# Two bottleneck blocks: relus of the last stage's first tile between the products, its last row in two halves, and the order of columns and quarters in the Gram stage

## Chip, cores and metric

The kernel runs on one core of one Trainium2 chip. The metric is the device time of one execution in microseconds; three executions of the kernel before took 1890.41, 1890.45 and 1893.24 us, with a median of 1890.45 us.

## What is computed

Two residual bottleneck blocks in a row on a batch of 64 images with 1024 channels of 14 x 14 pixels, in float32, with batch statistics:

```python
out = relu(bn(conv1x1(x, w1), g1, be1))      # 1024 -> 256 channels
out = relu(bn(conv3x3(out, w2), g2, be2))    # 256 -> 256
out = bn(conv1x1(out, w3), g3, be3)          # 256 -> 1024
x = relu(x + softplus(residual_scale)[0] * out)
```

`bn` takes mean and variance over the batch and all pixels, so every normalization needs a whole layer before it can begin.

## The kernel before

A tile is two images: 128 partitions by 8 slices of channels (`CS`) by 392 pixels (`PX`); there are 32 tiles (`T`). The 256 channels in the middle of a block stay in SBUF (`y_all`, two slots of 128). Each block runs as: first 1x1 convolution, 3x3 convolution, a stage that finds the statistics of the third convolution, and the third convolution with the residual. In the second block the statistics come from the Gram matrix of `y` (`gram`, line 1315, and `conv3_stats`, line 1747), and the third convolution is the last stage (`residual`, line 1804, and `final`, line 1834). The change lies in these two.

Four engines work in parallel, each through its own queue in order: TensorE (PE) multiplies, VectorE (DVE) and ScalarE (ACT) normalize, copy and add, GpSimd (POOL) adds and issues some transfers, SyncE (SP) issues most transfers. `matmul` (line 160) and `act` (line 335) are helpers, so all matmuls show line 160 and most of ACT's work line 335. Both pin their instruction to the order of the program; what isn't pinned is placed by a scheduler.

**Gram stage.** `gram` builds products of pixel-major pieces of `y`. A group of 256 pixels is turned either by TensorE (`by_tensor`, 1389: four transposes into PSUM, then a copy to a tile `zt`; it serves the three groups of the piece `turned`, 768 pixels) or by DVE (`by_vector`, 1408, with STREAM_TRANSPOSE at 1307; it serves the eight pieces in `moved`). DVE turns only 32 x 32 blocks, so a moved piece is first spread over partitions by transfers into a buffer `home` (`move`, 1377, on SP and POOL) and, for the blocks that keep their partitions, by four copies on ACT (`stay`, 1370). Before any of that a piece is normalized by ACT (`normed`, a relu with scale and shift) and has a constant subtracted by DVE (`less`, 1348, through `center` at 1346). The first two moved pieces go by quarters (`quarter_comes`, 1413): normalized, centred and moved one after the other, so that the first transfers start early. The generator `pairs` (1420) writes this order out by hand. First come tile 0 and the four products of the last stage's first tile that fit into PSUM (`conv3_begun`, `conv3`); then the columns of `turned` and the quarters; then one `yield` for each group of 256 pixels, after which `gram_products` (1286) multiplies the group before it.

**Last stage.** Tile 0's eight products (`made`) exist before the scales do: four were put into `z` and four lie in PSUM banks. `residual` adds each to `x_0` with DVE (line 1813: product times scale plus `x`) and lets ACT do the relu; then one store of `x_0` on POOL's queue. Tiles 1 to 30 follow in pairs, four units each (`Conv3Pair`, 652), by a scheme with seven products in place of eight (`Seven`, 246; `stream`, 290). The first two units are started together: `p1` of both, then `p2`, `p6`, `p5`, `p6`, `p7`. After `p1`, `p6` and `p7` ACT copies the bank `y` (tag `cy`) into a tile `cu`, and the next product adds into that bank after the copy has read it. After `p2` and `p5` DVE adds the bank `cx` or `cp` to `x` (line 532), and `p3` adds into `cp` after that. POOL adds the copies to `x` (555 and 663), ACT and DVE do the relus (`end`, 665, and `go_out`, 670), and SP stores each unit's slices (675). `x_6` uses the buffer of `x_0`, so its load on SP waits for `x_0`'s store. Tile 31 comes last, again through `residual`: eight products of 392 columns, each followed by DVE and a relu on ACT, stores of two slices and, for the last two, of one slice each.

Of the kernel before, what the change touches and what calls it, by code (L numbers as in the profile page):

```python
# [18 lines left out]
CS = C // P  # L19
MS = M // P  # L20
G = 2
# [49 lines left out]
def bottlenecks(ctx: ExitStack, tc: tile.TileContext, x, w1s, w2s, w3s, pars, out):  # L71
# [429 lines left out]
    class Conv3(Seven):  # L501
# [25 lines left out]
        def part(self, row, i):  # L527
            return self.xt[:, self.o[row], i * self.n : (i + 1) * self.n]
# [786 lines left out]
    def gram(psum, pool, homes, z, aff, minus_c, w3, beside):  # L1315
# [44 lines left out]
        def quarter(k, i):  # L1360
            a, e = moved[k]
            n = (e - a) // 4
            return a + i * n, a + i * n + n

        def home(k):
# [44 lines left out]
            turn(zt, home(k)[0], i * CH)  # L1410
            return zt

        def quarter_comes(k, i):
            normed(*quarter(k, i))
            less(*quarter(k, i))
            move(k, (i,))
# [387 lines left out]
    def residual(psum, xt, b, t, w3, aff, made=(), later=None):  # L1804

        scale, shift = aff
        to = mids[t] if b == 0 else out[t]
        tail = b == 1 and t == T - 1
        first = CS // 2 if b == 1 and t == 0 else 0
        for n, o in enumerate((*range(first, CS), *range(first))):  # L1810
            ps = made[o] if o < len(made) else conv3(psum, t, o, w3)
            v = xt[:, o, :]
            nc.vector.scalar_tensor_tensor(v, ps, scale[:, o : o + 1], v, ALU.mult, ALU.add)  # L1813
            relu = partial(act, v, v, AF.Relu, bias=shift[:, o : o + 1])
            if later is not None and o + 2 >= CS:
                later.append(relu)
            else:
                relu()

            step = CS if not tail else 1 if o + 2 >= CS else 2  # L1820
            if (n + 1) % step == 0:
                o = n
                queue = nc.scalar if o + 1 == CS and tail else nc.gpsimd if step == CS and b else nc.sync
                store = partial(
                    queue.dma_start,
                    out=to[:, (o + 1 - step) * PX : (o + 1) * PX],
                    in_=xt[:, o + 1 - step : o + 1, :].rearrange("p s f -> p (s f)"),
                )
                if later is not None:
                    later.append(store)  # L1830
                else:
                    store()

    def final(psum, pool, xpool, xs, a, w3, aff):


        units = []

        def pairs():
            for t in range(1, T - 1, 2):  # L1840
                ys = [[two(t + i, s) for i in range(2)] for s in range(MS)]
                sums = column_sums(pool, ys, PX, (2,))
                for q in range(CS // 2):
                    units.append(Conv3Pair(psum, pool, xs[t : t + 2], q, PX, ys, sums, w3, aff, out[t : t + 2]))
                    yield units[-1]

# [12 lines left out]

    def fused(psum, pool, one, right, coming, xs, raw, w1, w3, aff, par, stats, border, begun):  # L1860

# [323 lines left out]
    for b in range(2):  # L2185
# [9 lines left out]
        with tc.tile_pool(name=f"last_{b}", bufs=1, **({"reuse_waits": "tile"} if b == 0 else {})) as one, tc.tile_pool(  # L2195
# [12 lines left out]
            with ExitStack() as scope:  # L2208
# [41 lines left out]
                later = None if b else []  # L2250
                residual(psum, xs[0], b, 0, w3, aff, made, later)
                if b == 1:
                    more = scope.enter_context(tc.tile_pool(name="last_more", bufs=1, reuse_waits="tile"))
                    xs.append(load_x(more, b, len(xs), run=tc.keep_in_program_order))
                with tc.tile_pool(name=f"rest_{b}", bufs=1) as pool:
                    if b == 1:
                        final(psum, pool, [x_left] * 5 + [more], xs, w3, *weights, aff)
# [44 lines left out]
```

## Time and profile before

| | |
|---|---|
| runs | 1890.41, 1890.45, 1893.24 us, median 1890.45 us |
| the profiled execution | 1891.91 us, span from first to last instruction 1890.1 us |
| TensorE matmul busy | 1869.9 us (99%) |
| DVE, ACT, POOL busy | 1574.5 us (83%), 1106.6 us (59%), 740.0 us (39%) |
| TensorE's granted clock over the span | 0.998 |
| Gram stage of block 2 | 1509 to 1574 us of the span |
| last stage | 1588 to 1890 us of the span |

Times in the profile are microseconds from the span's start. A row of the timeline has start, duration, engine, line, operation, `out<-in` by tile names with the buffer numbers left out, shapes and a count; in brackets stand the idle time ahead of it on its engine and what ended that. Rows with a count are merged. A busy TensorE can still be at half clock; the table by stretches tells the clock that was granted.

### The profile page before, as it was taken

The numbers are of one execution on the slowest core, as the hardware profiler recorded it, in microseconds if no ns is written. First come the engines' busy times: TensorE is split into PE (matmuls) and PEld (weight loads), VectorE is DVE, ScalarE is ACT, GpSimd is POOL, SyncE is SP. The second block draws the span as 40 slices with busy tenths as digits, with TensorE's granted clock in tenths as the row PEclk, the third lists the DMA queues.
The fourth block names the chain that finished last, engine by engine and source line by source line (L and its number), as shares of the span: only waits on it lengthen the run. The fifth ranks groups of instructions, "written<-read, shape, count | busy, mean of one in ns | idle before, by whom it ended". The sixth has DMA issues, their size and how long they took to land. (4 is left out here: it accounts for less than half of the span.)

```text
span 1890.1 us, 28589 instructions
## 1 busy us (share of the span) xinstructions
PE 1869.9 (99%) x9748; PEld 1559.8 (83%) x9748; DVE 1574.5 (83%) x2498; ACT 1106.6 (59%) x2304; POOL 740.0 (39%) x762
## 2 busy tenths in 40 slices
PE   9999999999999999999999999999999999999999
PEld 5555557999998998899999999999999986555555
DVE  5787867999998776788788787899999986888886
ACT  2222214677777665555555555457777793666666
POOL 0111100211205655376776777311121151666664
PEclk9999999999999999999999999999999999999999
DMA  7777644787865556778787889468788376899997
GB/s 289 273 251 272 214 181 139 206 218 213 211 202 164 185 168 216 258 267 318 276 286 279 306 283 286 189 195 218 208 215 221 130 183 255 294 347 342 341 338 280
DMA packets 263186, 459.17 MB, mean 243 GB/s; under 512 B 59361, under 2 KB 229569, under 8 KB 249857
## 3 DMA queue, kind: packets, MB, share of 16 engines
q1 hardware_dynamic: 224784, 375.37, 59.5%
q0 software_dynamic: 31408, 29.30, 7.9%
q10 hardware_dynamic: 6848, 52.67, 6.8%
q8 instruction: 77, 1.26, 0.3%
q14 instruction: 69, 0.56, 0.1%
HBM read 289.44 MB, written 141.03 MB: 228 GB/s over the span
## 5 line engine op out<-in xcount | busy, mean ns | idle before, releaser
L160 PE MATMUL columns<-v,ub 128*128 128x224 f32 (+1 forms) x1536 | 302.9, 339 | 1.3 <-ACT columns L335 0.8
L335 ACT ACTIVATE x<-x,shift 128x392 f32<-128x392 f32 x452 | 259.8, 614 | 75.0 <-DVE x L532 31.4
L160 PEld LDWEIGHTS columns<-v,ub 128*128 128x128 f32 x1536 | 268.5, 188 | 8.0 <-ACT columns L335 1.5
L335 ACT ACTIVATE cu<-cy,scale 128x196 f32<-128x196 f32 (+1 forms) x360 | 175.6, 500 | 168.9 <-PE cy L160 161.9
L160 PE MATMUL ay<-at,ws 128*128 128x196 f32 (+1 forms) x760 | 191.5, 383 | 0.4 <-DVE at L453 0.2
L532 DVE SCALAR_TENSOR_TENSOR x<-cp,scale,x 128x196 f32<-128x196 f32 (+1 forms) x240 | 124.7, 520 | 50.6 <-PE cp L160 49.3
L160 PEld LDWEIGHTS ay<-at,ws 128*128 128x128 f32 x760 | 134.9, 190 | 35.5 <-ACT au L335 0.5
L663 POOL TENSOR_TENSOR x<-x,cu 128x392 f32<-128x392 f32 x120 | 125.6, 1047 | 73.9 <-DVE x L532 73.3
L335 ACT ACTIVATE au<-ay 128x196 f32<-128x196 f32 (+1 forms) x139 | 53.5, 385 | 169.7 <-PE ay L160 159.7
L160 PE MATMUL l<-diffs,ub 128*128 128x224 f32 (+1 forms) x768 | 149.7, 337 | 0.5 <-DVE diffs L801 0.3
L160 PE MATMUL m<-sums,ua 128*128 128x224 f32 (+1 forms) x752 | 146.0, 336 | 1.2 <-issue 0.6
L160 PEld LDWEIGHTS l<-diffs,ub 128*128 128x128 f32 x768 | 134.5, 189 | 1.7 <-DVE diffs L801 0.7
L160 PEld LDWEIGHTS m<-sums,ua 128*128 128x128 f32 x752 | 131.4, 189 | 2.6 <-issue 1.0
L1102 POOL DMA_DIRECT2D y<-f x24 | 32.2, 1644 | 256.3 <-DVE f L1001 256.3
L160 PE MATMUL cx<-y,w 128*128 128x196 f32 (+1 forms) x400 | 123.7, 395 | 0.0
L555 POOL TENSOR_TENSOR x<-x,cu 128x196 f32<-128x196 f32 (+1 forms) x120 | 104.5, 871 | 48.4 <-ACT cu L335 31.2
L160 PE MATMUL cy<-y,w 128*128 128x196 f32 (+1 forms) x372 | 116.1, 399 | 1.8 <-ACT y L335 0.9
L335 ACT ACTIVATE y<-y,shift,scale 128x320 f32<-128x320 f32 (+8 forms) x111 | 111.9, 1036 | 7.1 <-DVE shift L2055 6.4
L560 POOL TENSOR_TENSOR x<-x,cu 128x392 f32<-128x392 f32 x60 | 80.3, 1338 | 85.1 <-DVE x L532 83.6
L207 POOL DMA_DIRECT2D u<-y x48 | 26.0, 543 | 210.9 <-ACT y L335 210.1
L160 PE MATMUL cy<-ct,ws 128*128 128x392 f32 x240 | 100.7, 503 | 3.7 <-ACT cu L335 3.7
L1904 POOL TENSOR_SCALAR y<-y,scale 128x392 f32<-128x392 f32 x57 | 92.3, 1620 | 28.5 <-DVE scale L2245 28.5
(317 smaller groups left out, 4522.0 us busy)
## 6 DMA issues: line engine op xcount, KB each, us to landing
ub<-u SPq DMA_DIRECT2D x92, 768.0 KB, 5.7
x<-in_x SPq DMA_DIRECT2D x35, 1568.0 KB, 8.1
x<-mid SPq DMA_DIRECT2D x32, 1568.0 KB, 8.2
out<-x SPq DMA_DIRECT2D x123, 392.0 KB, 7.0
mid<-x ACTq DMA_DIRECT2D x30, 1568.0 KB, 8.6
x<-in_x SPq DMA_DIRECT2D x108, 392.0 KB, 7.9
ua<-u SPq DMA_DIRECT2D x92, 256.0 KB, 3.2
z<-kept SPq DMA_DIRECT2D x60, 392.0 KB, 2.9
```

Source lines behind the costliest of these rows:

```text
L160: tc.keep_in_program_order(nc.tensor.matmul(*args, **kw))
L207: nc.gpsimd.dma_start(out=us[b][i][:, s, o], in_=u)
L335: tc.keep_in_program_order(nc.scalar.activation(*args, **kw))
L532: run(nc.vector.scalar_tensor_tensor(v, bank, self.scale[:, o : o + 1], v, ALU.mult, ALU.add))
L555: run(nc.gpsimd.tensor_add(self.part(1, 1), self.part(1, 1), u3))
L560: run(nc.gpsimd.tensor_add(v, v, self.u12))
L663: nc.gpsimd.tensor_add(v, v, self.u12[:, i * self.n : (i + 1) * self.n])
L1102: nc.gpsimd.dma_start(out=out_rows[3][:, o], in_=fa[:, o, :full], accum_op=ALU.add)
L1904: run(nc.gpsimd.tensor_scalar(z, z, scale[:, o : o + 1], None, ALU.mult))
```

## The change

Three places.

1. *Tile 0 in the last stage.* `residual` now adds one slice and returns its relu. `final` makes the additions of slices 4 to 7 ahead of the units and those of slices 0 to 3 at the first four products, and issues one waiting relu at every second product; after the eighth it issues the store. Block 1's tile 0 keeps its order (`first_tile`).
2. *The end.* `ending` makes the eighth slice of tile 31 as two products of half the rows (196 columns), each with its own DVE operation, relu and store; the last store stays on ACT's queue.
3. *Gram stage.* `conv3_begun` and the other early products are written ahead of the quarters; the columns of `turned` stand after the second quarter of the first moved piece instead of after the fourth; the second moved piece goes by halves instead of quarters; the first subtraction on the third piece stands after the second transposed group instead of ahead of the first.

```diff
-            for i in range(4):
-                quarter_comes(0, i)
             for o, tag in enumerate(("cy", "cx") * 2):
                 made.append(conv3(psum, 0, o, w3, tag) if o else conv3_begun(psum, 0, o, w3, tag))
-            normed(*turned, (0,))
-            normed_less(y_all[:, 1, slice(*turned)], 1)
-            less(*turned, (0,))
-            quarter_comes(1, 0)
+            for i in range(4):
+                comes(0, i, 4)
+                if i == 1:
+                    normed(*turned, (0,))
+                    normed_less(y_all[:, 1, slice(*turned)], 1)
+                    less(*turned, (0,))
             yield by_tensor(0, "ax", None)
-            quarter_comes(1, 1)
-            normed(*quarter(1, 2))
+            comes(1, 0, 2)
             yield by_tensor(1, "cp", act)
-            less(*quarter(1, 2))
-            move(1, (2,))
-            quarter_comes(1, 3)
+            comes(1, 1, 2)
             yield by_tensor(2, "ax", None)
             normed(*moved[2])
             stay(1)
-            less(*moved[2], both[:1])
             for k, (a, e) in enumerate(moved):
                 for i in range((e - a) // px):
                     yield by_vector(k, i)
-                    if k + 2 < len(moved) and i in ((1,), (1, 3))[k > 0]:
-                        last = k == 0 or i == 3
-                        less(*moved[k + 2], both[last:][:1])
-                        if last:
+                    if k + 2 < len(moved) and i in (1, 3):
+                        less(*moved[k + 2], both[i // 2 :][:1])
+                        if i == 3:
                             move(k + 2)
...
+    def residual(xt, o, ps, aff, here=slice(0, PX)):
+        scale, shift = aff
+        v = xt[:, o, here]
+        nc.vector.scalar_tensor_tensor(v, ps, scale[:, o : o + 1], v, ALU.mult, ALU.add)
+        return partial(act, v, v, AF.Relu, bias=shift[:, o : o + 1])
...
+    def ending(psum, xt, w3, aff):
+        for o in range(CS):
+            parts = 2 if o + 1 == CS else 1
+            for i in range(parts):
+                rows = slice(i * H // parts, (i + 1) * H // parts)
+                here = slice(i * PX // parts, (i + 1) * PX // parts)
+                ps = psum.tile(PX // parts)
...
+                residual(xt, o, ps, aff, here)()
+                a = o - 1 if o % 2 and o + 1 < CS else o
+                if o % 2 or o + 2 == CS:
+                    queue = nc.scalar if o + 1 == CS and i + 1 == parts else nc.sync
...
-        for _ in stream(pairs(), (T // 2 - 1) * CS // 2, together=True):
-            pass
+        half = CS // 2
+        relus = [residual(xs[0], o, made[o], aff) for o in range(half, CS)]
+        for k, _ in enumerate(stream(pairs(), (T // 2 - 1) * CS // 2, together=True), 1):
+            if k <= half:
+                relus.append(residual(xs[0], k - 1, made[k - 1], aff))
+            if k % 2 == 0 and relus:
+                relus.pop(0)()
+                if not relus:
+                    nc.gpsimd.dma_start(out=out[0], in_=xs[0].rearrange("p s f -> p (s f)"))
         for unit in units:
             unit.go_out()
-        residual(psum, xs[T - 1], 1, T - 1, a, aff)
+        ending(psum, xs[T - 1], a, aff)
```

How the queues stand before and after, first on ACT where the last stage begins (`x_0` is tile 0, `x_1` and `x_2` the first pair, `cu` the copies of a unit's bank). Before:

```order
L335 ACTIVATE x_0_12274<-x_0_12274,shift 128x392 x8
L335 ACTIVATE cu_12317<-cy,scale 128x392
L335 ACTIVATE cu_12318<-cy,scale 128x392
L335 ACTIVATE cu_12317<-cy,scale 128x392
L335 ACTIVATE cu_12318<-cy,scale 128x392
L335 ACTIVATE cu_12336<-cy,scale 128x392
L335 ACTIVATE x_2_12278<-x_2_12278,shift 128x392
```

After, at the same place on ACT:

```order
L335 ACTIVATE cu_12296<-cy,scale 128x392
L335 ACTIVATE x_0_12266<-x_0_12266,shift 128x392
L335 ACTIVATE cu_12297<-cy,scale 128x392
L335 ACTIVATE x_0_12266<-x_0_12266,shift 128x392
L335 ACTIVATE cu_12296<-cy,scale 128x392
L335 ACTIVATE x_0_12266<-x_0_12266,shift 128x392
L335 ACTIVATE cu_12297<-cy,scale 128x392
L335 ACTIVATE cu_12322<-cy,scale 128x392
L335 ACTIVATE x_0_12266<-x_0_12266,shift 128x392
L335 ACTIVATE x_2_12270<-x_2_12270,shift 128x392
```

The first copy has moved ahead of all relus of `x_0`, and four of those stand among the first five copies; the other four stand by twos among the next units' copies. DVE's queue keeps its order here: eight additions to `x_0`, then the first unit's additions.

On DVE in the Gram stage (`y` 128x320 and 128x640 are quarters and halves of moved pieces, 128x768 the columns of `turned`, 128x1536 the third moved piece, `ax` the bank of TensorE's transposes, `home` a moved piece). Before:

```order
L1346 TENSOR_SCALAR y<-y,minus_c 128x320 x8
L1358 TENSOR_SCALAR y<-y,scale,shift 128x768
L1358 TENSOR_SCALAR y<-y,minus_c 128x768
L1346 TENSOR_SCALAR y<-y,minus_c 128x768
L1346 TENSOR_SCALAR y<-y,minus_c 128x320 x2
L1405 COPY zt_11482<-ax 128x2x256
L1346 TENSOR_SCALAR y<-y,minus_c 128x320 x6
L1405 COPY zt_11484<-ax 128x2x256
L1346 TENSOR_SCALAR y<-y,minus_c 128x1536
L1307 STREAM_TRANSPOSE zt_11485<-home 128x2x256
```

After, at the same place on DVE:

```order
L1346 TENSOR_SCALAR y<-y,minus_c 128x320 x4
L1358 TENSOR_SCALAR y<-y,scale,shift 128x768
L1358 TENSOR_SCALAR y<-y,minus_c 128x768
L1346 TENSOR_SCALAR y<-y,minus_c 128x768
L1346 TENSOR_SCALAR y<-y,minus_c 128x320 x4
L1405 COPY zt_11482<-ax 128x2x256
L1346 TENSOR_SCALAR y<-y,minus_c 128x640 x4
L1405 COPY zt_11484<-ax 128x2x256
L1307 STREAM_TRANSPOSE zt_11485<-home 128x2x256
L1307 STREAM_TRANSPOSE zt_11486<-home 128x2x256
L1346 TENSOR_SCALAR y<-y,minus_c 128x1536
```

The three operations on the columns have moved ahead of four of the eight 320-wide ones, and two transposed groups ahead of the 1536-wide one. TensorE's own queue keeps its order in both places; it differs only in the last row of tile 31.

More of the change, by code (lines that the diff above doesn't have):

```diff
@@ L1358, in normed_less, with part @@
                 tc.keep_in_program_order(nc.vector.tensor_scalar(y, y, value, more, op, last))
-        def quarter(k, i):
+        def part(k, i, parts):
             a, e = moved[k]
-            n = (e - a) // 4
+            n = (e - a) // parts
             return a + i * n, a + i * n + n
@@ L1411, in by_vector, with comes @@
             return zt
[L1413 to L1416, printed above, removed]
+        def comes(k, i, parts):
+            normed(*part(k, i, parts))
+            less(*part(k, i, parts))
+            n = 4 // parts
+            move(k, range(i * n, i * n + n))
         made = []
@@ L1802, in conv3_stats @@
         nc.vector.tensor_sub(mv[:, :, 1], mv[:, :, 1], sq)
-    def residual(psum, xt, b, t, w3, aff, made=(), later=None):
+    def residual(xt, o, ps, aff, here=slice(0, PX)):
         scale, shift = aff
[L1807 to L1815, printed above, removed]
-                later.append(relu)
[L1817 to L1832, printed above, removed]
@@ L1834, in final, with first_tile @@
-    def final(psum, pool, xpool, xs, a, w3, aff):
+        v = xt[:, o, here]
+        nc.vector.scalar_tensor_tensor(v, ps, scale[:, o : o + 1], v, ALU.mult, ALU.add)
+        return partial(act, v, v, AF.Relu, bias=shift[:, o : o + 1])
+    def first_tile(psum, xt, to, w3, aff, made):
+        later = []
+        for o in range(CS):
+            relu = residual(xt, o, made[o] if o < len(made) else conv3(psum, 0, o, w3), aff)
+            if o + 2 < CS:
+                relu()
+            else:
+                later.append(relu)
+        later.append(partial(nc.sync.dma_start, out=to, in_=xt.rearrange("p s f -> p (s f)")))
+        return later
@@ new lines, in ending @@
+    def ending(psum, xt, w3, aff):
+        for o in range(CS):
+            parts = 2 if o + 1 == CS else 1
[3 more added lines that the diff above has]
+                ps = psum.tile(PX // parts)
+                for s in range(MS):
+                    matmul(
+                        ps.rearrange("p (h l) -> p h l", l=G * W), w3[:, s, o, :], two(T - 1, s)[:, rows],
+                        start=s == 0, stop=s == MS - 1,
+                    )
+                residual(xt, o, ps, aff, here)()
+                a = o - 1 if o % 2 and o + 1 < CS else o
+                if o % 2 or o + 2 == CS:
+                    queue = nc.scalar if o + 1 == CS and i + 1 == parts else nc.sync
+                    queue.dma_start(
+                        out=out[T - 1][:, a * PX + here.start : o * PX + here.stop],
+                        in_=xt[:, o, here] if a == o else xt[:, a : o + 1].rearrange("p s f -> p (s f)"),
+                    )
@@ L1837, in final @@
+    def final(psum, pool, xpool, xs, made, a, w3, aff):
         units = []
@@ L2249, in bottlenecks @@
                     xs = [load_x(x_left, b, t, run=tc.keep_in_program_order) for t in range(5)]
-                later = None if b else []
-                residual(psum, xs[0], b, 0, w3, aff, made, later)
+                if b == 0:
+                    later = first_tile(psum, xs[0], mids[0], w3, aff, made)
                 if b == 1:
@@ L2256, in bottlenecks @@
                     if b == 1:
-                        final(psum, pool, [x_left] * 5 + [more], xs, w3, *weights, aff)
+                        final(psum, pool, [x_left] * 5 + [more], xs, made, w3, *weights, aff)
                         return
```

## The prediction

> **What bounds the kernel now.** I read the page's totals first (span 1890.1 us), then the waits of TensorE, then the timeline around each wait.
>
> ```profile
> PE 1869.9 (99%) x9748; PEld 1559.8 (83%) x9748; DVE 1574.5 (83%) x2498; ACT 1106.6 (59%) x2304; POOL 740.0 (39%) x762
> ```
>
> TensorE (PE) is busy for 99% of the span, so only two things can shorten the run: TensorE waiting less, or its matmuls running faster. The waits from 1505 us to the end, which hold all three places that the change touches, are five:
>
> ```profile
> PE cy L160 <- ACT cu L335: 3.7, 1, 3.7
> PE cy L160 <- ACT y L335: 0.9, 1, 0.9
> PE cp L160 <- DVE zt L1307: 0.9, 1, 0.9
> PE ax L1395 <- DVE y L1346: 0.6, 1, 0.6
> PE cp L160 <- DVE zt L1405: 0.4, 1, 0.4
> ```
>
> Columns: who waited for whom, total us, times, longest. The first wait opens the last stage, the other four open the Gram stage; from 1594 us to the end TensorE never waits. The busy time hides something else, which the table by stretches shows (TensorE busy, its granted clock, DMA share, GB/s):
>
> ```profile
> 1592.00:1594.00 2.00, 0.16 (x1) 0.76 0.46 88
> ...
> 1598.00:1600.00 2.00, 2.00 (x5) 0.53 0.89 326
> 1600.00:1602.00 2.00, 2.00 (x8) 1.00 1.03 439
> ```
>
> After the 3.7 us wait TensorE is "busy", but at half clock until almost 1600 (0.53 of two us means 1.88 us at half, so until 1599.9). That one wait costs twice.
>
> **Part 1, opening of the last stage.** TensorE, ScalarE (ACT) and VectorE (DVE) there:
>
> ```profile
> 1589.37 0.82 PE L160 MATMUL cx<-y,w 128*128 128x392 f32 x2
> 1593.84 1.68 PE L160 MATMUL cy<-ct,ws 128*128 128x392 f32 x2 [3.66 <-ACT cu L335]
> 1599.23 1.14 PE L160 MATMUL cp<-y,ws 128*128 128x392 f32 x2
> 1600.21 0.83 PE L160 MATMUL cy<-ct,w 128*128 128x392 f32 x2
> 1600.88 0.82 PE L160 MATMUL cx<-y,w 128*128 128x392 f32 x2
> ```
>
> ```profile
> 1588.95 4.37 ACT L335 ACTIVATE x<-x,shift 128x392 f32<-128x392 f32 x8 [3.65 <-DVE x L1813]
> 1593.22 1.04 ACT L335 ACTIVATE cu<-cy,scale 128x392 f32<-128x392 f32 x2
> ```
>
> ```profile
> 1590.43 2.23 DVE L1813 SCALAR_TENSOR_TENSOR x<-z,scale,x 128x392 f32<-128x392 f32 x4
> 1592.58 0.62 DVE L532 SCALAR_TENSOR_TENSOR x<-cx,scale,x 128x392 f32<-128x392 f32 x1
> 1596.87 0.63 DVE L532 SCALAR_TENSOR_TENSOR x<-cp,scale,x 128x392 f32<-128x392 f32 x1 [3.67 <-PE cp L160]
> ```
>
> The first `cu` copy, which TensorE needs before it may add into `cy` again, stands behind eight relus of `x_0` (4.37 us). In the changed order it stands ahead of them. A product takes 0.66 us at full clock (1600.21 to 1600.88) and drains 0.16 longer (0.82). The `cy` products of both units directly precede `cx` at 1589.37, so the first is complete about 1588.9, its copy runs 1588.9 to 1589.5, and TensorE goes on from `cx` without a wait: the next four (`cy`, `cp`, `cy`, `cy`) stand at 1590.03, 1590.69, 1591.35 and 1592.0. ACT can serve them: copies at 0.5 to 0.6 us with one relu of 0.54 us (4.37 over eight) between puts the third copy, for the product at 1592.0, at about 1590.9 to 1591.5.
>
> The next product (`cp`, 1599.23 before) is then late for another reason. It adds into a bank that DVE must have read first, and on DVE the eight `x_0` operations keep their place ahead: the last four, started 0.54 us apart, end at 1592.66 (1590.43 + 2.23), `cx` follows at 1592.58 and, another 0.54 later, `cp` at 1593.12 to 1593.74. So this product starts at 1593.80, after a new wait of about 1.0 us, instead of at 1599.23: **5.4 us earlier**. As a check: the wait of 3.66 goes, 1.0 comes, and the four products that took 1599.23 − 1593.84 = 5.39 us fall to 4 × 0.66 = 2.64, which gives 2.75; 3.66 − 1.0 + 2.75 = 5.4. It needs the clock to stay up through the 1.0 us wait, as it did through 0.9 and 0.6 us in the Gram stage:
>
> ```profile
> 1516.00:1524.00 8.00, 6.38 (x74) 5.15 (x76) 6.68 (x15) 7.98 (x11) 3.51 (x7) 1.00 1.02 202
> ```
>
> (the third figure from the end is the clock). From the row 1592:1594 the clock fell at about 1593.0 (0.76 of 2 us means 0.96 us at half), 2.85 us after the last matmul ended at 1590.19.
>
> The Trainium skill ("TensorE: Matmul & The Clock Gate", Part 1) says that a cold array becomes warm after about 3.4 us of sustained work, which would make the half-clock loss 1.7 us; the trace shows about 6 us of it and a loss of 2.75, and the measurement decides. By the page alone the sum below would be 1.05 us smaller.
>
> What moves with it: four relus still stand on ACT among the second unit's and third unit's copies. By the same steps a copy for the second unit's last product comes 0.1 us late; I take **5.3 us**, with bounds 3.5 (ACT late by up to three more relus of 0.54) and 5.8 (no new DVE wait for half of the way). The store of `x_0` moves on GpSimd's queue (POOL) from 1593.6 behind six adds, to about 1600.5; on SP the load of `x_6`, which needs that buffer, falls behind the first unit's two stores. I cost this at nothing, since the first use of `x_6` on DVE, now at 1635.52, would come at about 1630; the price without that cover is the third rival.
>
> **Part 2, Gram stage.** Same engines:
>
> ```profile
> 1516.32 0.63 PE L1395 MATMUL ax<-ident,y 128*128 128x128 f32 x4 [0.60 <-DVE y L1346]
> 1523.02 0.55 PE L160 MATMUL cp<-zt 128*64 128x193 f32 x4 [0.89 <-DVE zt L1307]
> ```
>
> ```profile
> 1515.56 1.21 DVE L1346 TENSOR_SCALAR y<-y,minus_c 128x768 f32<-128x768 f32 x3
> 1517.05 0.69 DVE L1405 COPY zt<-ax 128x512 f32<-128x512 f32 x1 [0.29 <-PE ax L1395]
> 1520.07 0.69 DVE L1405 COPY zt<-ax 128x512 f32<-128x512 f32 x1
> 1521.32 1.02 DVE L1346 TENSOR_SCALAR y<-y,minus_c 128x1536 f32<-128x1536 f32 x1 [0.57 <-ACT y L335]
> 1522.26 1.30 DVE L1307 STREAM_TRANSPOSE zt<-home 128x512 f32<-128x512 f32 x2
> 1532.36 1.30 DVE L1307 STREAM_TRANSPOSE zt<-home 128x512 f32<-128x512 f32 x2 [1.12 <-ACT home L335]
> ```
>
> ```profile
> L335 ACT ACTIVATE y<-y,shift,scale 128x320 f32<-128x320 f32 x16 | 9.0, 638 | 0.0
> L335 ACT ACTIVATE y<-y,shift,scale 128x768 f32<-128x768 f32 x1 | 1.0, 1012 | 0.0
> ```
>
> The transposes wait for the 768-wide subtraction, which now stands behind all four quarters. Moved ahead of two quarters it is due some 2 us earlier, about 1514.0, before TensorE ends its four opening products. That removes 0.60, and 0.16 of pipeline overlap: transposes at 1515.56. The first copy still waits for them, and the matmuls behind it come 0.76 earlier. The second copy (1520.07) now stands behind four 640-wide subtractions whose relus end, by ACT's work as summed below, about 1519.0, so it starts at about 1519.45, 0.6 earlier.
>
> Then the large piece: the first transposition by DVE (1522.26) stands behind a 1536-wide subtraction that waits for ACT. In the change it follows the copy directly, at 1520.15, if its 16 transfers have landed. The last of them:
>
> ```profile
> home<-y SPq DMA_DIRECT2D x2, 80.0 KB, 4.6
> ```
>
> The later of these is issued at 1516.01 and lands about 1520.1; two of its quarters are now centred after the columns, 0.9 us later on DVE, of which SP's queue, with one issue each 0.6 us, takes up some: I put that issue 0.6 later. So the transposition starts about 1520.85 and TensorE's products at 1521.6 instead of 1523.02: 1.4 us.
>
> Not all of it stays. ACT does not rest here (7.98 of 8.00 us in the row of 1516:1524); eight 320-wide relus become four 640-wide ones. By the group rows (638 and 1012 ns for 320 and 768 columns) a relu takes 0.83 ns per column, and sixteen of 638 ns keep ACT busy for only 9.0 us, so each starts 0.08 before the one ahead of it ends; two of 320 take 1.1 and one of 640 takes 0.82 us; four times 0.28 is 1.1 us saved, less 0.3 in which ACT now waits for the second transposes: 0.8. The row at 1532.36 shows DVE waiting for ACT's own-quarter copies; those come 0.8 earlier, and the third piece's transfers start 0.7 later, because its subtraction moves behind the transpositions. There the lead shrinks to about **1.1 us**. Bounds: 0.4 (the transfers land a further 0.7 late) and 1.6.
>
> **Part 3, the end.**
>
> ```profile
> 1885.79 0.63 DVE L1813 SCALAR_TENSOR_TENSOR x<-cx,scale,x 128x392 f32<-128x392 f32 x1 [0.69 <-PE cx L160]
> 1886.45 0.62 ACT L335 ACTIVATE x<-x,shift 128x392 f32<-128x392 f32 x1 [0.69 <-DVE x L1813]
> ```
>
> ```profile
> L532 DVE SCALAR_TENSOR_TENSOR x<-cp,scale,x 128x392 f32<-128x392 f32 x120 | 74.8, 623 | 30.9 <-PE cp L160 29.8
> L532 DVE SCALAR_TENSOR_TENSOR x<-cp,scale,x 128x196 f32<-128x196 f32 x120 | 49.9, 416 | 19.7 <-PE cp L160 19.5
> ```
>
> ```profile
> out<-x SPq DMA_DIRECT2D x1, 392.0 KB, 2.5
> out<-x SPq DMA_DIRECT2D x1, 196.0 KB, 1.9
> ```
>
> TensorE ends at the same time, since two half-width sets are as many columns. Behind it stand half a DVE operation (623 to 416 ns: −0.21), half a relu (0.62 less 196 × 0.83 ns: −0.16) and a store of 98 KB. Halving 392 KB took 0.6 off the landing, so another halving gives 0 to 0.3; I take 0.1, the nearer row being 1.9 already. Sum: **0.5 us**, bounds 0.3 and 0.7.
>
> The Trainium skill ("DMA: Bandwidth & Descriptors", Anatomy of one DMA) has a constant 2.0 us for a transfer and bytes only behind it, which speaks against halving a store: by it the 0.1 would be under 0.25 and mostly nothing. It leaves the sum where it is.
>
> **Sum.** 5.3 + 1.1 + 0.5 = 6.9 us. The profiled execution took 1891.91 us (span 1890.1), so it would take 1885.0; it lies 1.46 above the median of the runs shown, 1890.45, and from that median the forecast is **1883.5 us**. By the bounds the gain lies between 4.2 and 8.1.
>
> **Rivals.**
> - *The clock falls all the same.* If the new wait for DVE grew from 1.0 to 2.85 us, the product would start at 1595.7 and most of the half-clock loss of 2.75 would return: 3.5 − 2.7 = 0.8 there, 2.4 in all, 1888.0. Against it: the DVE queue ahead is known by rows and unchanged in order; two waits of 0.9 left the clock at 1.00. Chance 0.10.
> - *Gram gives nothing and ACT is crowded.* ACT is without rest in the one place and gets 3 to 4 extra relus in the second and third unit in the other. If Gram keeps 0.4 and the last stage 4.3, the sum is 5.2: 1885.3. Chance 0.11.
> - *Slower: `x_6` comes late.* One mechanism: SP's load of `x_6` must await the landing of `x_0`'s store, and SP issues nothing past it.
>
> ```profile
> x<-mid SPq DMA_DIRECT2D x2, 1568.0 KB, 11.5
> out<-x POOLq DMA_DIRECT2D x1, 1568.0 KB, 13.5
> ```
>
> ```profile
> 1635.52 0.61 DVE L532 SCALAR_TENSOR_TENSOR x<-cp,scale,x 128x392 f32<-128x392 f32 x1
> ```
>
> (the last row is the first use of `x_6`). Issued at 1600.5, with 13.5 us for the store and 11.5 for the load, `x_6` is there at 1625.5, before 1630. Each us later than 1630 is a us of TensorE. It decides from about 1634: a wait of 4.2 plus 2.75 at half clock eats the 6.9, and landing at 1637 would end near 1893. Against it: 13.5 was measured with two loads beside it, which will have landed. Chance 0.05.
>
> **How the numbers follow.** The forecast (gain 5.5 to 8.1) has 0.74, the rivals 0.10, 0.11 and 0.05. About 0.2% (3.8 us) is what a measurement of this kernel can tell from no change. The forecast, the second rival and a quarter of the first lie beyond it: faster 0.88; the rest of the first, 0.07, is the same; slower 0.05. The range reaches from 1881.8 (8.1 gained and half a us of scatter) to 1886.5 (4.2 gained, rounded outward), and leaves out the first and third rival.
>
> **What would show it.** Right: no wait of TensorE over 1.5 us after 1510; a wait of about 1 us for DVE `x` L532 some 3 us into the last stage's first unit; granted clock 1.00 there; first Gram products of a transposed piece about 1.4 us earlier, and 1.1 by the end of Gram; about 0.4 us from the last matmul's end to the last store's issue less than now. Wrong: a stretch at 0.50, TensorE waiting for `x` by DMA near the ninth unit, or new waits for `cu` in units two and three.

## The result, and the profile after

The changed kernel takes **1886.17 us** (median of 10 runs, 1884.92 to 1887.57), the kernel before 1890.89 beside it (10 runs, 1889.70 to 1893.24): a ratio of 0.9973, 95% interval 0.9963 to 0.9983, so 4.7 us less, within 3.2 and 7.0. The forecast, 1883.5 in a range of 1881.8 to 1886.5, had the sign and, near its upper end, the time; it promised 2.7 us too much. The profiled execution took 1886.21 us, its span 1884.4 instead of 1890.1.

The page's totals of the changed kernel first, then TensorE's waits from 1505 us to the end (who waited for whom, total us, times, longest):

```profile
PE 1867.1 (99%) x9752; PEld 1558.0 (83%) x9752; DVE 1572.2 (83%) x2495; ACT 1105.2 (59%) x2301; POOL 740.6 (39%) x762
```

```profile
PE cp L160 <- DVE zt L1307: 1.5, 2, 1.4
PE cp L160 <- DVE x L532: 1.0, 1, 1.0
PE cy L160 <- ACT y L335: 0.9, 1, 0.9
PE cp L160 <- DVE zt L1405: 0.4, 1, 0.4
```

The 3.7 us wait for `cu` is gone, and so is the 0.6 us wait of the transposes. Two things are new: the 1.0 us wait for DVE, as forecast, and a 1.4 us wait for DVE's transposed columns, which was not forecast.

**Opening of the last stage.** TensorE, ScalarE and VectorE of the changed kernel, then its table by stretches:

```profile
1591.79 1.48 PE L160 MATMUL cy<-ct,ws 128*128 128x392 f32 x4
1594.23 0.93 PE L160 MATMUL cp<-y,ws 128*128 128x392 f32 x2 [0.97 <-DVE x L532]
```

```profile
1589.49 0.59 ACT L335 ACTIVATE cu<-cy,scale 128x392 f32<-128x392 f32 x1 [3.75 <-DVE x L1805]
1589.98 0.61 ACT L335 ACTIVATE x<-x,shift 128x392 f32<-128x392 f32 x1
1590.49 0.58 ACT L335 ACTIVATE cu<-cy,scale 128x392 f32<-128x392 f32 x1
```

```profile
1590.88 2.23 DVE L1805 SCALAR_TENSOR_TENSOR x<-z,scale,x 128x392 f32<-128x392 f32 x4
...
1593.57 0.61 DVE L532 SCALAR_TENSOR_TENSOR x<-cp,scale,x 128x392 f32<-128x392 f32 x1
```

```profile
1590.00:1592.00 2.00, 2.00 (x7) 1.15 (x7) 2.00 (x5) 2.00 (x6) 0.00 (x0) 1.00 0.11 44
1592.00:1594.00 2.00, 1.27 (x4) 0.38 (x2) 2.00 (x5) 1.84 (x5) 0.21 (x1) 1.00 0.00 0
1594.00:1596.00 2.00, 1.77 (x6) 1.07 (x7) 0.95 (x3) 0.60 (x2) 1.87 (x3) 1.00 0.97 257
```

Copies and relus alternate on ScalarE, TensorE runs on, and its product at 1594.23 waits 0.97 us for the addition that DVE starts at 1593.57, behind the eight of `x_0`. The clock (third figure from the end) stays at 1.00. From the last `cx` product to this one TensorE took 9.54 us before (1589.69, the second matmul of the row at 1589.37, to 1599.23) and takes 4.09 now (1590.14 to 1594.23): 5.45 us less. Up to the end of TensorE's last matmul the difference is 5.47 (296.06 and 290.59 us).

**Gram stage.** Some rows of TensorE, VectorE and SP's queue:

```profile
1521.50 0.55 PE L160 MATMUL cp<-zt 128*64 128x193 f32 x4
...
1534.05 0.55 PE L160 MATMUL cp<-zt 128*64 128x193 f32 x4 [1.37 <-DVE zt L1307]
```

```profile
1520.73 1.30 DVE L1307 STREAM_TRANSPOSE zt<-home 128x512 f32<-128x512 f32 x2 [0.44 <-DMA home<-y]
1521.96 0.98 DVE L1346 TENSOR_SCALAR y<-y,minus_c 128x1536 f32<-128x1536 f32 x1
1522.85 1.30 DVE L1307 STREAM_TRANSPOSE zt<-home 128x512 f32<-128x512 f32 x2
1524.07 0.98 DVE L1346 TENSOR_SCALAR y<-y,minus_c 128x1536 f32<-128x1536 f32 x1
...
1533.29 1.30 DVE L1307 STREAM_TRANSPOSE zt<-home 128x512 f32<-128x512 f32 x2 [2.68 <-PE ap L160]
```

```profile
1525.08 7.48 SPq L1384 DMA_DIRECT2D home<-y  x11
```

Before, SP's row at this place was:

```profile
1524.49 8.06 SPq L1384 DMA_DIRECT2D home<-y  x10
```

The first transposed columns reach TensorE at 1521.50 instead of 1523.02: the lead is there. Twelve us later it is gone: the third piece's transposition, at 1532.36 before, starts at 1533.29. The releaser named, PE `ap`, is not it: TensorE has nothing left to do from 1532.7. The landings in the trace show the third piece's last packets at 1532.62 (before: 1531.38); of VectorE's own wait instructions, which follow one another 0.1 us apart, the last that took longer ended at 1532.69, right behind that landing. In all five traces of this order the transposition starts 0.67 us behind the last landing. So the transfers are last now, where ScalarE was before.

**The end.** TensorE's last row, the last relu and the last store's issue:

```profile
1879.90 0.83 PE L160 MATMUL cy<-y,w 128*128 128x196 f32 x4
```

```profile
1881.22 0.46 ACT L335 ACTIVATE x<-x,shift 128x196 f32<-128x196 f32 x1 [0.15 <-DVE x L1805]
1881.71 0.34 ACTq L1838 DMA_DIRECT2D out<-x  x1
```

Before, TensorE's last row and the last store's issue were:

```profile
1884.28 1.48 PE L160 MATMUL cx<-y,w 128*128 128x392 f32 x4
1887.11 0.34 ACTq L1832 DMA_DIRECT2D out<-x  x1
```

The last matmul ends at 1880.73 (before 1885.76), so the issue is done 1.32 us behind it instead of 1.69, and the span ends 3.67 us behind it instead of 4.34.

### The profile page after: what moved, and what is told of

The parts are those of the page before. It is cut to its first block, busy times and chain, and to the rows that moved or that the text cites. A ratio compares the mean times of both kernels' runs of the same rounds, so it can differ in the third digit from the quotient of the medians.

```text
span 1884.4 us, 28588 instructions
## 1 busy us (share of the span) xinstructions
PE 1867.1 (99%) x9752; PEld 1558.0 (83%) x9752; DVE 1572.2 (83%) x2495; ACT 1105.2 (59%) x2301; POOL 740.6 (39%) x762
## 4 chain that ended last, share of the span: by engine, by line
PE 90%; DVE 5%; ACT 2%; DMA 1%; issue 1%; POOL 0%; SPq 0%; ACTq 0%; DVEq 0%; POOLq 0%
PE ay L160 20%; PE cy L160 16%; PE columns L160 13%; PE ap L160 11%; PE cp L160 9%; PE m L160 6%; PE l L160 6%; PE cx L160 4%; PE ax L160 4%; PE ps L160 1%; DMA home<-y 1%; ACT y L335 1%; DVE zt L1307 0%; DMA x<-in_x 0%; DVE f L1001 0%
## 5 line engine op out<-in xcount | busy, mean ns | idle before, releaser
L335 ACT ACTIVATE y<-y,shift,scale 128x320 f32<-128x320 f32 (+9 forms) x107 | 110.8, 1061 | 7.1 <-DVE shift L2071 6.4
L961 ACT ACTIVATE columns<-m 128x448 f32<-128x448 f32 (+1 forms) x144 | 70.8, 492 | 55.4 <-PE m L160 48.6
```

Source lines behind the costliest of these rows:

```text
L335: tc.keep_in_program_order(nc.scalar.activation(*args, **kw))
L961: copy(v, m, AF.Copy)
```

## Experiments

The theory that I held after the result: the gain is the last stage's opening (wait and clock) and the end; the Gram stage gives nothing because its third piece starts later. Each trace is of one execution; places are compared by lengths within one trace, since the Gram stage's start lies between 1509.4 and 1511.3 us in them. The kernels were timed in four sets, each with runs of before beside it, whose medians differ (1890.62 to 1891.39 us); where a difference of about 1 us between kernels of two sets matters, the traces decide.

### The opening alone

Before with the new `final`; the Gram stage as before, `ending` with the last row whole. Against the changed kernel, besides the Gram stage's old lines:

```
-            parts = 2 if o + 1 == CS else 1
+            parts = 1
```

> Only the opening of the last stage is changed; Gram and the end stand as before. Theory A (the opening is worth its wait and its half-clock stretch, 3.66 - 0.97 + 2.75, as the profiles of before and after suggest): 5.4 us less than before, about 1885.5; in the trace one wait of about 1.0 us for DVE x, no stretch at half clock, and everything up to 1589 where before has it. Rival (only the wait counts, the slow products are slow for another reason): 2.7 us less, 1888.2.

Measured: 1886.59 us (10 runs, 1886.38 to 1887.44) beside 1891.39 (20 runs), ratio 0.9975 (0.9965 to 0.9984): 4.8 us less. The rival's 2.7 us is a ratio of 0.9986, outside the interval. One wait of 0.97 us for DVE, no slow stretch: theory A, 0.6 us short of its 5.4. That shortfall has a cause, found below.

### The Gram change alone

> Only the Gram stage's new order; last stage and end as before. Theory A (the lead is real but is given back where the third moved piece lands late): TensorE about 1.5 us ahead of before at 1530, level again from 1534, and 0 to 0.5 us behind from 1548 on; time within 0.5 us of before. Rival, as the prediction had it: 1.1 us ahead at the end of Gram, time 1.1 less than before.

Measured: 1891.35 us (11 runs) beside 1891.39, ratio 1.0000 (0.9991 to 1.0009). From the first product of the stage (1511.32) to the last `cx` product (1590.85) TensorE took 79.52 us, against 79.70 in before. Five traces of the new order (this, after, and three kernels below that keep it) gave 79.52 to 80.02 us, mean 79.72; six of the old order gave 79.70 or 79.71 five times and 80.16 once. So the new order is worth nothing, and the forecast's 1.1 us falls.

This trace showed something else. Its opening is that of before, and has the wait of 3.66 us; yet the products behind it ran at full clock:

```profile
1594.99 0.93 PE L160 MATMUL cy<-ct,ws 128*128 128x392 f32 x2 [3.66 <-ACT cu L335]
1595.76 0.82 PE L160 MATMUL cp<-ct,ws 128*128 128x392 f32 x2
```

```profile
1592.00:1594.00 2.00, 0.00 (x0) 0.00 (x0) 2.00 (x5) 2.00 (x5) 0.00 (x0) 1.00 0.00 0
1594.00:1596.00 2.00, 1.01 (x3) 0.68 (x4) 0.35 (x1) 1.46 (x4) 1.17 (x2) 1.00 0.69 138
```

Two matmuls take 0.82 us here; in the profile of before they took 1.68. The same wait does not always cost the clock: up to the end of TensorE's last matmul this trace takes 293.35 us from the last `cx` product, against 296.06.

### The third piece earlier

After, with the third piece's subtractions one transposition earlier each, its transfers behind the second transposition instead of the fourth:

```
-                    if k + 2 < len(moved) and i in (1, 3):
-                        less(*moved[k + 2], both[i // 2 :][:1])
-                        if i == 3:
+                    if k + 2 < len(moved) and i in ((0, 1), (1, 3))[k > 0]:
+                        last = i == (1, 3)[k > 0]
+                        less(*moved[k + 2], both[last:][:1])
+                        if last:
```

> After, with the third piece's two subtractions one transposition earlier each, and its transfers issued behind the second transposition by DVE instead of the fourth. Theory A (those transfers are late because they start late): first issue at about 1524.1 instead of 1525.08, the transposition that took 1533.29 at about 1532.3, TensorE's wait of 1.37 down to about 0.4, and the kernel 0.8 to 1.3 us faster than after. Rival B (the transfers are slowed by other traffic, so their start does not matter): the transposition stays at 1533.0 to 1533.3 and the time within 0.3 of after. Rival C (ScalarE's own-quarter copies, ending at 1531.69, would be next): the gain stops at 1531.7, as A at most 1.4.

VectorE, SP's queue and ScalarE of this kernel:

```profile
1522.72 0.98 DVE L1346 TENSOR_SCALAR y<-y,minus_c 128x1536 f32<-128x1536 f32 x1
...
1531.60 1.30 DVE L1307 STREAM_TRANSPOSE zt<-home 128x512 f32<-128x512 f32 x2 [1.12 <-ACT home L335]
```

```profile
1523.72 9.67 SPq L1384 DMA_DIRECT2D home<-y  x11
```

```profile
1528.16 3.41 ACT L335 ACTIVATE home<-y 32x768 f32<-32x768 f32 x4
```

Measured: 1884.95 us (5 runs, 1884.65 to 1885.64), ratio to before 0.9968 (0.9955 to 0.9980), 1.2 below after's median. The transfers start 1.36 us earlier than in after, the last packets land at 1530.88 instead of 1532.62, and the transposition starts as ScalarE's copies end, 1.69 earlier. TensorE's wait of 1.4 us is gone, and the stage takes 78.87 us, 0.83 less than before; the last stage takes what it takes in after (290.59 us from the last `cx` product to the end of TensorE's last matmul). So B falls, and A holds up to the point that C named: ScalarE is last again, though hardly: with the 0.67 us that lie between landing and transposition, the transfers were due at 1531.55, and it started at 1531.60.

### The additions of z behind the first unit

The wait of 0.97 us comes from DVE's order. Here the four additions that read `z` stand behind the first unit's two, and the order on DVE is pinned there:

```
+            if k == 1:
+                pinned.append(True)
+            if k == 14:
+                pinned.clear()
-            if k <= half:
-                relus.append(residual(xs[0], k - 1, made[k - 1], aff))
+            if k in (6, 8, 10, 12):
+                n = (6, 8, 10, 12).index(k)
+                relus.append(residual(xs[0], n, made[n], aff))
...
-                if not relus:
+                if not relus and k >= 12:
```

(the last lines keep the store of `x_0` behind the last of these additions)

> After, with the four additions of x_0 that read z put behind the first unit's additions on DVE (the order there pinned). Theory A (the 0.97 us wait in the opening is only DVE's queue ahead of the addition that frees the bank): that wait goes, everything behind comes 0.9 to 1.0 us earlier, 1885.2. Rival (ScalarE's relus and copies are then late, since the relus of x_0 wait for these additions): a wait for cu of 0.5 to 1.0 us takes its place, time as after.

TensorE and VectorE of this kernel:

```profile
1591.49 1.48 PE L160 MATMUL cy<-ct,ws 128*128 128x392 f32 x4
1592.80 0.82 PE L160 MATMUL cp<-y,ws 128*128 128x392 f32 x2
```

```profile
1591.69 0.63 DVE L532 SCALAR_TENSOR_TENSOR x<-cp,scale,x 128x392 f32<-128x392 f32 x1 [0.49 <-PE cp L160]
1592.23 1.16 DVE L1805 SCALAR_TENSOR_TENSOR x<-z,scale,x 128x392 f32<-128x392 f32 x2
```

Measured: 1885.06 us (5 runs, 1884.50 to 1885.81), 1.1 below after. The product follows without a wait, 2.96 us behind the last `cx` product instead of 4.09. Behind it two products start 0.18 and 0.17 us late, the first of them for a `cu` copy; up to the end of TensorE's last matmul 0.93 us are left (289.66 against 290.59). That is theory A; the rival's wait of 0.5 to 1.0 us did not come.

### Both together

> After, with both edits that gained alone: the third piece's subtractions one transposition earlier, and the additions of x_0 that read z behind the first unit's. Theory A (they act at two places 60 us apart and add up): 1.2 and 1.0 us less than after, 1884.0, and no wait of TensorE over 0.5 us from 1512 to the end. Rival (the earlier end of Gram only lets the next engine wait, DVE's chain into the last stage): the gain of one of them alone, 1885.0.

Measured: **1884.06 us** (5 runs, 1883.52 to 1884.61), ratio to before 0.9966 (0.9952 to 0.9979), 2.1 below after's median; expected 1884.0. Of TensorE's waits from 1505 us on, these are left:

```profile
PE cy L160 <- ACT y L335: 0.9, 1, 0.9
PE cp L160 <- DVE zt L1405: 0.4, 1, 0.4
PE cp L160 <- DVE zt L1307: 0.4, 2, 0.2
```

The two gains add up, as the trace shows: the Gram stage takes 78.83 us (78.87 with the third piece's edit alone), and from the last `cx` product to the end of TensorE's last matmul it is 289.68 us (289.66 with the other edit alone, 290.59 in after). The medians alone do not settle it: measured against the before of its own set, the kernel with the third piece's edit is 6.4 us faster, the one with `z` 6.3 and the one with both 6.6.

### The last row whole

After, with `parts = 1` in `ending`.

> After, with the last row in one piece again, as in before. Theory A (the halved row shortens what stands behind the last matmul by about 0.6 us): from the end of the last matmul to the end of the span 4.3 us as in before instead of 3.7, the median 0.5 to 0.7 above after, 1886.8. Rival (the last store's constant cost hides it, or more matmul starts cost TensorE as much): 0 to 0.2 above after.

Its last relu and last store's issue:

```profile
1881.45 0.62 ACT L335 ACTIVATE x<-x,shift 128x392 f32<-128x392 f32 x1 [0.70 <-DVE x L1805]
1882.10 0.34 ACTq L1838 DMA_DIRECT2D out<-x  x1
```

Measured: 1886.83 us (11 runs, 1885.74 to 1888.40), 0.66 above after. By the medians alone that is within the runs' scatter; the traces are finer. The last matmul ends at 1880.75, the issue at 1882.44, 1.69 later, and the span at 1885.1, 4.35 later, against 3.67 in after. Theory A: the halved row gives 0.37 up to the issue, and the store, 98 KB instead of 196, another 0.3.

### Six relus ahead of the first copy

After, with six of `x_0`'s eight relus issued before the stream of units, to lengthen the wait.

```
+        for relu in relus[:6]:
+            relu()
+        del relus[:6]
```

(with all eight additions made ahead of it)

> After, with six of the eight relus of x_0 ahead of the first cu copy on ScalarE instead of none. TensorE should wait about 2.6 us for cu there instead of 0.97 for DVE. Theory A (a wait shorter than about 2.8 us leaves the clock up): no stretch at half clock, 1.6 us slower than after, 1887.8. Rival (the clock falls with any wait of some us): a stretch of 6.8 us at half clock in the trace and 3.5 to 4.4 us slower than after, 1890.

Measured: 1887.82 us (10 runs, 1886.82 to 1889.23), 1.65 above after; expected 1887.8. TensorE:

```profile
1592.36 0.93 PE L160 MATMUL cy<-ct,ws 128*128 128x392 f32 x2 [2.59 <-ACT cu L335]
1593.12 0.82 PE L160 MATMUL cp<-ct,ws 128*128 128x392 f32 x2
```

A wait of 2.59 us left the clock at 1.00 in this trace, and by the median the wait alone was paid for, us for us. But the three longest of the ten runs (1889.02 to 1889.23 us) are the three whose mean clock is 0.999 and not 1.000, so in some executions this wait may still have cost clock; no trace of one is kept.

### The wait filled

Before, with matmuls in the 3.66 us whose result nobody reads:

```
+            if k == 3:
+                ps = psum.tile(PX, "ax")
+                for _ in range(9):
+                    matmul(ps.rearrange("p (h l) -> p h l", l=G * W), a[:, 0, 0, :], two(1, 0), start=True, stop=True)
```

> Before, with nine matmuls whose result nobody reads (into the bank that DVE has just read, ax) put on TensorE in the 3.66 us wait; the wait for the first cu copy itself stays. Theory A (the products behind the wait run slow because the granted clock falls when TensorE rests too long, and in the executions in which it falls this costs up to 2.75 us): the product after the wait still starts about 3.6 us late, no stretch at half clock in any execution, the median about 2 us below before, 1889.3, and the spread of the runs narrower than before's 3.8 us. Rival (the slow products have another cause than the rest): the median within 0.5 us of before. Second rival (the fillers delay the product themselves): later than before by what they stick out, up to 1 us.

Measured: 1891.83 us (11 runs, 1891.48 to 1892.49), ratio 1.0005. I had counted a filler as one matmul of 0.33 us; it is two. The nine ran until the product at 1595.80, 6.37 us behind the last `cx` product instead of 4.15, so the second rival applied, with 2.2 us where it had "up to 1 us". The spread, 1.0 us instead of before's 5.1, already pointed at the clock, but the number of fillers had to be smaller:

```
-                for _ in range(9):
+                for _ in range(4):
```

> Before with four fillers instead of nine, since each filler is two matmuls and takes 0.66 us, so that nine stuck out by 2.4 us. They should end 1.0 us before the cu copy is there. Theory A (the half-clock stretch comes from TensorE's rest): wait of about 1.0 us behind the fillers, the product after it where before has it, no stretch, all runs within 1.5 us of one another, the median 1.3 to 2.1 below before. Rival (the stretch is not due to the rest): as before within 0.4, with the same spread.

```profile
1590.25 2.90 PE L160 MATMUL ax<-y,w 128*128 128x392 f32 x8
1594.06 0.93 PE L160 MATMUL cy<-ct,ws 128*128 128x392 f32 x2 [0.91 <-ACT cu L335]
1594.82 0.82 PE L160 MATMUL cp<-ct,ws 128*128 128x392 f32 x2
```

Measured: **1889.40 us** (11 runs, 1888.73 to 1890.39) beside 1891.03 (15 runs, 1889.10 to 1893.45), ratio 0.9990 (0.9981 to 0.9999). The product still starts 4.15 us behind the last `cx` matmul, as in before, no useful work moved, and 1.6 us are gone with most of the spread. This is the clock's share by itself, as a mean over executions.

### Before, two more traces

> The kernel before, unchanged, for a second look at its wait of 3.66 us. Theory A (the clock is set in windows of 3.41 us, as the lengths of the clock's stretches suggest, all whole multiples of it, and falls after a window that is mostly rest): whether the products behind the wait run at half clock depends on where the windows' edges lie; with the wait cut by an edge so that both windows are over 35% busy there is no stretch and the span is near 1887.7, else a stretch of 3.4 or 6.8 us and a span of 1889 to 1891. Rival (a wait of 3.66 us always costs the stretch): 6.8 us at half clock in every look.

> The kernel before, unchanged, a third look; the same expectations as for the second.

The tables by stretches of the two, the second trace of before first:

```profile
1592.00:1594.00 2.00, 0.65 (x2) 0.49 (x3) 0.71 (x2) 1.78 (x4) 0.81 (x2) 1.00 0.58 100
1594.00:1596.00 2.00, 2.00 (x5) 1.01 (x4) 0.56 (x1) 0.59 (x1) 0.78 (x1) 0.58 1.01 351
1596.00:1598.00 2.00, 2.00 (x5) 1.05 (x4) 0.07 (x1) 0.60 (x2) 0.00 (x0) 0.56 0.86 238
```

```profile
1592.00:1594.00 2.00, 0.45 (x1) 0.37 (x2) 0.91 (x2) 1.98 (x4) 0.61 (x2) 0.93 0.47 82
1594.00:1596.00 2.00, 2.00 (x4) 1.01 (x3) 0.00 (x0) 0.59 (x1) 0.98 (x1) 0.50 0.85 307
1596.00:1598.00 2.00, 2.00 (x6) 1.07 (x5) 0.62 (x1) 0.47 (x1) 0.00 (x0) 0.71 0.99 270
```

A clock of 0.58 over two us means 1.68 us at half, 0.56 means 1.76: 3.4 us in the second trace, from 1594.3 to 1597.75. In the third: 0.28, 2.0 and 1.16 us, again 3.4, from 1593.7. The first profile had 6.8. So the rival falls: the same wait (3.66, 3.65, 3.66 us) costs one step of 3.41 us, two, or in the Gram kernel's trace none. From the last `cx` product to the end of TensorE's last matmul the four took 293.35 (none), 295.08 and 295.04 (one step) and 296.06 us (two). The spans of the two new traces were 1888.6 and 1888.8 us, a little under the 1889 to 1891 that theory A had.

## Why the prediction was right, and where it failed

By the two profiled executions, 1891.91 − 1886.21 = 5.7 us: 5.45 from the opening, 0.67 from the end, −0.32 from the Gram stage (79.70 to 80.02), and −0.13 because the stage started that much later.

**Part 1, the opening (forecast 5.3, bounds 3.5 to 5.8): right in its mechanism and, for that execution, in its size.** The wait of 3.66 went, 0.97 came in its place at the product and for the addition that were named (1.0 forecast), the clock stayed up, and the product came 4.09 us behind `cx` instead of 9.54. ScalarE's extra relus in the next two units cost next to nothing: one product starts 0.18 us late, at 1599.13, behind a `cu` copy that stands behind five relus, a gap too short for the table of waits. But the half-clock loss of 2.75 was the profiled execution's own. Over twenty runs of before, nine had a mean clock of 0.998 (1891.67 to 1893.32 us), nine 0.999 (1890.35 to 1892.51), and two 1.000 (1889.48 and 1889.57). This mean also counts the rest behind the last matmul, so it does not tell the loss of a single run: the trace of the Gram change alone has 0.999 without a slow stretch in the opening. The filled wait puts the mean loss at 1.6 us, the opening alone at 4.8 − 2.69 = 2.1. The step **"it lies 1.46 above the median of the runs shown, and from that median the forecast is 1883.5 us"** took a loss that one execution had in full from a median in which it is there in part: 0.7 to 1.1 us too much.

The Trainium skill ("TensorE: Matmul & The Clock Gate", Part 1) has the clock decided in free-running windows of 3413 ns, by how busy the array was. The stretches of 3.4 and 6.8 us agree, one window and two; so the prediction's remark that the trace and the Trainium skill differ rested on a trace with two windows.

**Part 2, the Gram stage (forecast 1.1, bounds 0.4 to 1.6): the step that failed, outside its bounds.** The early part held: transposes 0.76 earlier on their stage's own clock (1515.68, where before's 1516.32 would be 1516.44), and the first transposed product 1.65 earlier by the same reckoning (1.4 forecast). It failed at **"the third piece's transfers start 0.7 later … There the lead shrinks to about 1.1 us"**. They did start 0.6 later (1525.08 for 1524.49), as forecast. But I let ScalarE's copies stay last there, as they were before, and did not ask how much room the transfers had behind them. Before, they landed at 1531.38, and the transposition waited for ScalarE until 1532.36; with 0.67 us between landing and transposition that left 0.3 us of room, and with the lead wanted the transposition would have had to start near 1531. The transfers cannot start later and have the piece there earlier. They landed 1.24 later, and of the lead of 1.65 us on the stage's own clock 0.06 was left behind the third piece. At the fifth piece this execution lost another 0.39 (to 0.33 behind before); of the other four traces of this order one lost 0.20 there, the rest nothing. Started in time, the same new order gives 0.83 (third piece earlier): what the forecast missed is the place of one subtraction and twelve transfers, not the rest of the chain. Why landing slipped by 1.24 when the start slipped by 0.6 is not settled. SP issued its last of the seven no later than before (1528.91 for 1529.11), but it took 3.7 us to land instead of 2.3; GpSimd issued its last 1.1 us later (1527.96 for 1526.87). That the fourth piece's transfers, issued from 1530.0 on, get in their way is only argued.

**Part 3, the end (forecast 0.5, bounds 0.3 to 0.7): right,** 0.37 at the issue and 0.3 at the store, of which 0.1 had been taken and 0.3 was the bound. Two half-width sets took TensorE as long as one whole slice, as assumed: the last two rows of TensorE start 0.66 us apart, at 1879.24 and 1879.90, and whole slices 1.32. The section of the Trainium skill that the prediction names there ("DMA: Bandwidth & Descriptors", Anatomy of one DMA) gives its constant for transfers that GpSimd issues; this store is ScalarE's.

**The sum.** For 5.3 + 1.1 + 0.5 = 6.9 from the median the runs show about 4.8 (the opening alone) + 0 + 0.67 = 5.5, and 4.7 measured directly, whose interval reaches from 3.2 to 7.0. Of the 2.2 missing, 1.1 or more is Gram, and most of the rest the clock's mean loss. Both terms erred to the same side; that the time still lies inside the forecast's range, 0.3 us from its upper end, is owed to the width of the range and not to the second part.

**The rivals.** The first (the clock falls all the same) did not come: 1.00 through the new wait, and a mean clock of 1.000 in all ten runs. The second came in half: Gram gave nothing, for another reason than the crowded ScalarE it named, and the last stage kept its gain. The third (`x_6` late) did not come; the table of waits has none of TensorE behind 1594.23, and the store that it hung on landed quickly:

```profile
out<-x POOLq DMA_DIRECT2D x1, 1568.0 KB, 6.2
```

That is half of the 13.5 us that I had taken from before, where two loads ran beside it.

## What to carry to other kernels

When an edit brings a chain forward, take each input of its last step in turn and ask how much room that one had: the wait's named releaser tells only who was last, and here the next one had 0.3 us of room and had been moved the wrong way. A loss that may differ from execution to execution, such as a stretch at half clock, is priced over several executions before it is taken from a median: the runs' spread is a sign (2.8 us in the three runs of before that the prediction had, 3.8 in twenty, 1.1 with the opening alone). And of two orders that both free a queue, the one that also keeps the next consumer's operation first is better: four additions put behind two were worth another 0.93 us in the trace.

## What the runs showed of the hardware

The granted clock changes at the edges of a grid of 3.413 us: in the three traces of before it stood at 1.00 for 465 such steps (1587.2 us), then at 0.50 for one or two (3.41 or 6.83 us), then at 1.00 for 85 (290.1 us). The steps' place against the program differs between executions, and with it the price of one and the same wait. With the wait laid on that grid, the clock fell after a step in which TensorE was busy 5% (third trace of before), 16% (the first) and 29% of the time (the second); it did not after steps with 50 and 43% (the Gram change alone), 58 and 66% (six relus) or 72% (after). It came back after one step that was busy throughout; after one with 77%, in the first trace of before, it stayed at half for a second. These are few points; the limits lie somewhere between 29 and 43%, and between 77 and 100%. By them a wait of 2.59 us that falls into one step whole would leave it 24% busy (an estimate from the grid and the wait), which would cost clock; the three slower runs with six relus ahead would fit that, but no trace shows it. Shown is that here a wait of 3.66 us costs 0, 1.7 or 2.7 us on top of itself, as the grid falls, and that one of 0.97 us cost nothing on top in four traces.
